# How many tiles of the gated pairs' experts go out with each state of the first two half-sequence scans

## The chip, the cores and the metric

The kernel runs on one core of a Trainium2 chip. The metric is device time in microseconds, the median of several runs. Engine names are those of the profile: PE (TensorE matmuls) and PEld (its weight loads), DVE (VectorE), ACT (ScalarE), POOL (GpSimd), and SP, the engine whose queue issues most of the transfers. Everything is in float32.

## What is computed

The reference is a network of four layers on an input of 4 sequences x 1024 positions x 128 features. Each layer is a mixer and a feed-forward, each followed by a residual sum and a layer norm. The change concerns the last three of these eight steps.

The feed-forward of the third layer ("gated pairs": each token goes to two of eight gated experts):

```python
logits = x @ router_w.T;  probs = softmax(logits)
weights, indices = top_k(probs, 2);  weights /= weights.sum() + 1e-6
gate, up = split(x @ w13[e]);  y_e = (silu(gate) * up) @ w2[e]
out = sum over the two chosen e of weight_e * y_e
```

The mixer of the fourth layer, a selective state recurrence ("Recurrence") with 256 channels and 16 states per channel:

```python
h = exp(d_l[:, :, None] * A) * h + (d_l * x_l)[:, :, None] * b_l[:, None, :]
y_l = einsum('ben,bn->be', h, c_l)      # for every position l
```

Its input is the rms-normed stream, put through a projection, a causal convolution of width 4 and a silu; `d_l` is a softplus. Its output is gated with the silu of a skip projection and projected back to 128 features.

The feed-forward of the fourth layer has eight experts of width 512, and every token's sum is over all eight with a gate that is zero for those outside its top-p set. The kernel computes all eight for every token.

## The kernel before

**The program.** A Python program writes out every instruction. A planner then makes, from that stream, one fixed order for each engine: an instruction's place in the stream is its priority, buffers are taken from pools with a fixed number of slots, and the planner's own timing decides which of the ready instructions comes next. On the chip each engine runs its list in that order. So the place at which a piece of work stands in the stream decides where it stands on PE, ACT, DVE, POOL and SP. Work that overlaps is written as Python generators, and the loop that calls `next` on them sets how they are mixed.

**The gated pairs' experts: `l2_ffn`, lines 1402 to 1437.** A router sorts each sequence's 2 x 1024 token copies by expert into at most 23 tiles of 128 rows (`NT2`), so the four sequences have 92 tiles. The scatter of rows is an indirect transfer issued by POOL (line 1383), 16 of them a sequence. `l2_ffn` is a generator that works as a pipeline over a step number t: at step t it loads rows for tile t+8 (once in four tiles, `xg`, line 1442), the expert's weights for tile t+4 (`wx`, 384 KB, line 1458, four buffers), transposes rows for tile t+2 (once in four), computes the hidden layer of tile t (`ph`, `sg`, `mh`, lines 1474 to 1494) and the output of tile t-2 (`py`, `ys`, line 1498), which SP stores once in four tiles. It then yields. A step whose rows belong to a sequence that isn't scattered yet does nothing but yield:

```python
while t + 8 < n and "put" not in units[max(t + 8, 0)]["st"]:
    ...
    yield
```

When the last tile of a sequence is out, `l2_combine` (line 1519) runs as a side generator, two of its steps to a step of tiles (one, once the tiles are all out or while they wait for rows): 8 indirect gathers on POOL (`yg`, line 1529), weighted sums on ACT and DVE, a norm, and the same again for the sequence's second half. `yg` has one buffer.

**The recurrence: `l3`, from line 1595.** Each sequence is cut into two halves of 512 positions, which makes 8 half sequences. For each, `l3_prepare` (line 1714) computes the channels, `dl` and `ud`, and two sets of 16 rows, b and c, which go to DRAM. Then `l3_scan` (line 1815) goes over the 16 states. For one state SP loads `bn` and `cn` (a row spread over 128 partitions, 256 KB each, line 1840, four buffers each); POOL multiplies `db` = `ud` x `bn` (line 1845); ACT makes the decay `da` (line 1849); DVE runs the scan over time in two pieces (line 1850); POOL multiplies `hc` = `db` x `cn` (line 1861); PE sums `hc` over the states into `pys` through an identity matmul. From the second sequence on, two states' `hc` are first added by a transfer that POOL issues (line 1865). `l3_sum` and `l3_finish` (lines 1874 and 1886) gate, project, norm and route a half sequence; `l3_finish` puts it on the list `todo`.

**The last layer's experts: `l3_experts`, `l3_ffn` (lines 1638 and 1955).** A half sequence on `todo` is taken up when it has been there for more than three states. Each of its eight experts takes six steps of the generator `work`: four for the hidden pieces (`ph`, `hh`), two for the output (`py`) and its gated sum into `h_acc`. The weights `wh` are 512 KB an expert.

**What mixes them.** With every state of a scan, the loop in `l3` calls one step of the finish of the half before (`end`), one step of the preparation of the next half (`nxt`), one step of the last sequence's scatter (`self.m2["rest"]`), the steps of tiles (`moe`), and three steps of `work`, or four once the tiles are through. The tiles, `l3_prepare`, `l3_finish` and the last layer's experts all take their PSUM banks from one pool of four (`ff`). Before a scan whose next half begins a new sequence, the loop drains `moe` until that sequence is combined.

Most of the loop's tiles are of the third and fourth sequences. By the trace's tile names the first 45 hidden layers run before the recurrence's pools are made, and 47 after.

Of the kernel before, what the change touches and what calls it, by code (L numbers as in the profile page):

```python
# [58 lines left out]
class Net:  # L59
# [1535 lines left out]
    def l3(self, moe, fp):  # L1595

        c3 = self.c3  # L1600
        halves = [dict(b=b, h=h) for b in range(B) for h in range(2)]
        for i, u in enumerate(halves):
            u["prev"] = halves[i - 1] if u["h"] else None
        halves[0] = dict(self.c3["first"], **{k: halves[0][k] for k in ("prev",)})
        for i, u in enumerate(halves[1:], 1):
            u["prev"] = halves[i - 1] if u["h"] else None
        work = self.l3_experts(fp)
        end = iter(())
        for i, u in enumerate(halves):
            nxt = iter(())  # L1610
            if i + 1 < len(halves):
                if halves[i + 1]["h"] == 0:
                    while "done" not in self.m2["st"][halves[i + 1]["b"]]:
                        next(moe)
                nxt = self.l3_prepare(halves[i + 1])
            for f in self.l3_scan(u):
                next(end, None)
                next(nxt, None)
                for k in range(1):
                    next(self.m2["rest"], None)  # L1620
                busy = next(moe, moe) is not moe
                if i == 0:
                    for k in range(1):
                        next(moe, None)
                for k in range(3 if busy else 4):
                    next(work)
                for v in c3["todo"]:
                    v["age"] += 1
            for f in chain(end, nxt):
                pass  # L1630
            end = chain(self.l3_sum(u), self.l3_finish(u))
        for f in end:
            next(work)
        c3["all"] = True
        for f in work:
            pass
# [566 lines left out]
```

## Time and profile before

| | us |
|---|---|
| time before, median of 3 runs | 2328.13 (2327.18 to 2331.37) |
| profiled execution, its own time | 2329.42 |
| span of that execution | 2327.6 |
| PE busy, share of the span | 1994.8 (86%) |
| DVE busy | 1348.4 (58%) |
| ACT busy | 1205.4 (52%) |
| POOL busy | 1024.8 (44%) |
| first `db` multiply of the first scan | 1386.6 |
| last `hc` multiply of the eighth scan ends | 2176.6 |

"Busy" is the time in which an engine has an instruction in flight; on PE this includes the pipeline, so a PE that is called busy need not be at its peak. Shares over the whole span mix the layers; what counts for this change is the stretch from 1340 on. A stretch's own table (busy time of each engine between two times) shows which engine sets the pace there, and a wait is read as: this instruction stood still so long, and that is what ended it. "SPq" and "POOLq" are the queues on which SP and POOL issue transfers: what waits at the head of such a queue holds all that stands behind it.

The first multiplies of the eight scans start at 1386.6, 1471.8, 1562.1, 1661.6, 1777.8, 1879.7, 1989.5 and 2089.5. The hidden layers of the last 47 tiles run from 1352 to 1696.

### The profile page before, as it was taken

The numbers are of one execution on the slowest core, as the hardware profiler recorded it, in microseconds if no ns is written. First come the engines' busy times: TensorE is split into PE (matmuls) and PEld (weight loads), VectorE is DVE, ScalarE is ACT, GpSimd is POOL, SyncE is SP. The second block draws the span as 40 slices with busy tenths as digits, with TensorE's granted clock in tenths as the row PEclk, the third lists the DMA queues.
The fourth block names the chain that finished last, engine by engine and source line by source line (L and its number), as shares of the span: only waits on it lengthen the run. The fifth ranks groups of instructions, "written<-read, shape, count | busy, mean of one in ns | idle before, by whom it ended". The sixth has DMA issues, their size and how long they took to land. (4 is left out here: it accounts for less than half of the span.)

```text
span 2327.6 us, 46367 instructions
## 1 busy us (share of the span) xinstructions
PE 1994.8 (86%) x17802; PEld 1395.0 (60%) x17802; DVE 1348.4 (58%) x3693; ACT 1205.4 (52%) x2617; POOL 1024.8 (44%) x813
## 2 busy tenths in 40 slices
PE   6667979979999999999979857678898989889888
PEld 3455655544477777787767654355655556546556
DVE  7458743433445554654655557767776767776421
ACT  6543433332244444454565556566668766666343
POOL 5000230000123244234143259989887887769300
PEclk9757979979999999999999978889999989899899
DMA  3000110014000010031222176457765666666421
GB/s 105 0 19 18 31 38 6 14 40 140 1 3 2 3 37 22 25 88 42 84 77 72 49 221 182 146 165 204 219 175 162 180 173 163 180 164 177 100 59 50
DMA packets 138701, 211.62 MB, mean 91 GB/s; under 512 B 18613, under 2 KB 75952, under 8 KB 138096
## 3 DMA queue, kind: packets, MB, share of 16 engines
q1 hardware_dynamic: 126192, 173.87, 24.7%
q0 software_dynamic: 12288, 34.79, 7.2%
q8 instruction: 140, 2.29, 0.4%
q14 instruction: 81, 0.66, 0.1%
HBM read 160.29 MB, written 23.16 MB: 79 GB/s over the span
## 5 line engine op out<-in xcount | busy, mean ns | idle before, releaser
L1059 POOL TENSOR_TENSOR qt<-r_q,sb_c_turn 128x256 f32<-128x256 f32 (+1 forms) x256 | 164.4, 663 | 446.7 <-ACT r_q L1051 441.0
L1861 POOL TENSOR_TENSOR hc<-db,cn 128x1024 f32<-128x1024 f32 x128 | 311.3, 2453 | 64.4 <-PE pys L127 20.4
L1845 POOL TENSOR_TENSOR db<-ud,bn 128x1024 f32<-128x1024 f32 x112 | 283.7, 2597 | 30.6 <-DVE pmv L159 19.1
L127 PEld LDWEIGHTS py<-wh,hh 128*128 128x128 f32 x2048 | 251.8, 196 | 67.8 <-issue 38.7
L127 PE MATMUL ph<-xT,wh 128*128 128x512 f32 x512 | 262.5, 634 | 21.7 <-ACT hh L1973 8.0
L127 PE MATMUL py<-wh,hh 128*128 128x128 f32 x2048 | 257.2, 280 | 13.0 <-ACT hh L1973 10.1
L1973 ACT ACTIVATE hh<-ph,sb_cols 128x512 f32<-128x512 f32 x256 | 170.6, 682 | 146.2 <-PE ph L127 119.9
L1117 DVE TENSOR_TENSOR a<-pa_m,sb_c_near 128x256 f32<-128x256 f32 x256 | 96.6, 419 | 204.2 <-PE pa_m L127 204.2
L1074 ACT ACTIVATE kN<-kp_mo,sb_c_trig 128x128 f32<-128x128 f32 x448 | 130.2, 372 | 131.9 <-PE kp_mo L131 122.1
L1849 ACT ACTIVATE da<-dl,aneg 128x512 f32<-128x512 f32 x224 | 153.2, 689 | 84.1 <-DVE db L1850 83.3
L127 PE MATMUL pys<-hc,sb_c_ident 128*128 128x512 f32 x320 | 162.0, 636 | 24.6 <-POOL hc L1861 15.0
L1850 DVE TENSOR_TENSOR_SCAN db<-da,carry,db 128x512 f32<-128x512 f32 x128 | 156.8, 1266 | 25.9 <-ACT da L1849 12.5
L127 PEld LDWEIGHTS ph<-xT,wh 128*128 128x128 f32 x512 | 93.5, 202 | 115.0 <-issue 65.7
L1850 DVE TENSOR_TENSOR_SCAN db<-da,db 128x512 f32<-128x512 f32 x128 | 149.1, 1205 | 14.3 <-ACT da L1849 8.2
L1989 DVE SCALAR_TENSOR_TENSOR h_acc<-py,gt,h_acc 128x128 f32<-128x128 f32 x256 | 71.9, 342 | 140.4 <-PE py L127 140.4
L127 PE MATMUL pqk<-xT,wE 128*128 128x256 f32 x512 | 137.7, 393 | 8.2 <-ACT coT L1193 4.2
L127 PEld LDWEIGHTS pys<-hc,sb_c_ident 128*128 128x128 f32 x320 | 61.7, 206 | 90.0 <-issue 59.1
L127 PEld LDWEIGHTS pqk<-xT,wE 128*128 128x128 f32 x512 | 89.4, 195 | 22.1 <-DVE cv L1036 8.1
L729 POOL DMA_INDIRECT orows<-o,ix x20 | 18.9, 946 | 185.3 <-DVE o L727 158.8
L131 PE MATMUL pt<-sb_c_ident,xN 128*128 128x128 f32 x224 | 54.5, 345 | 52.1 <-ACT xN L174 33.9
L1193 ACT COPY coT<-pt 128x512 f32<-128x512 f32 x64 | 37.6, 587 | 114.7 <-PE pt L131 114.7
L127 PE MATMUL po<-ht,wD 128*128 128x512 f32 x192 | 93.7, 595 | 0.0
(457 smaller groups left out, 4342.4 us busy)
## 6 DMA issues: line engine op xcount, KB each, us to landing
wx<-in_wF SPq DMA_DIRECT2D x92, 384.0 KB, 3.4
bn<-rows SPq DMA_DIRECT2D x128, 256.0 KB, 4.9
cn<-rows SPq DMA_DIRECT2D x128, 256.0 KB, 4.5
wh<-in_wH SPq DMA_DIRECT2D x64, 512.0 KB, 3.9
hc<-hc POOLq DMA_DIRECT2D x48, 512.0 KB, 7.1
xrows<-zero SPq DMA_DIRECT2D x4, 1472.0 KB, 12.4
xg<-xrows SPq DMA_DIRECT2D x20, 256.0 KB, 3.1
yrows<-ys SPq DMA_DIRECT2D x20, 256.0 KB, 3.3
```

The costliest lines, as they stand in the source:

```text
L127: return self.nc.tensor.matmul(out=out, lhsT=lhsT, rhs=rhs, start=start, stop=stop)
L131: self.nc.tensor.transpose(out, in_, self.ident[0:n, 0:n])
L1059: nc.gpsimd.tensor_mul(u["qt"][:, m, a:], u["q"][:, a:], c2["turn"][:, m, o + a : o + 2 * P])
L1074: self.nc.scalar.activation(u["kN"][:, c, m, :], pk[:, c, :], AF.Copy, scale=trig[:, k, m : m + 1])
L1117: nc.vector.tensor_mul(u["a"][:, i, :, :], pa[i], self.c2["near"][:, None, :].to_broadcast([P, 2, P]),)
L1193: nc.scalar.copy(oT, pt)
L1845: nc.gpsimd.tensor_mul(db, ud, bc[0])
L1849: nc.scalar.activation(da, dl[:, ec, :], AF.Exp, scale=aneg[:, j : j + 1])
L1850: nc.vector.tensor_tensor_scan(db[:, ec, :], da, db[:, ec, :], carry[:, ec, n : n + 1] if h else 0.0, ALU.mult, ALU.add,)
L1861: nc.gpsimd.tensor_mul(hc, db, bc[1])
L1973: nc.scalar.activation(ht, ph, AF.Relu, bias=self.col("h_b1", i=e * NK + k))
L1989: nc.vector.scalar_tensor_tensor(acc[:, c, :], py[:, c, :], gt[:, c, e : e + 1], acc[:, c, :], ALU.mult, ALU.add,)
```

## The change

In the loop of `l3`, i is the number of the half sequence, 0 to 7. Before, one step of tiles goes out with each state, and one more in half sequence 0. After, three more go out in half sequence 0 and one more in half sequence 1: four and two steps a state, and one in the others, as before.

```diff
                 for k in range(1):
                     next(self.m2["rest"], None)
                 busy = next(moe, moe) is not moe
-                if i == 0:
-                    for k in range(1):
-                        next(moe, None)
+                for k in range((3, 1)[i] if i < 2 else 0):
+                    next(moe, None)
                 for k in range(3 if busy else 4):
                     next(work)
```

## Prediction

> **What bounds the kernel now.** I read first the page's busy shares, then a table of busy time by stretch, then waits and queues inside the stretches that the change reaches. A "scan" below is the sixteen states of one half sequence; I cut the trace where each scan's first POOL multiply `db` starts. The columns are time, then busy PE, PEld, DVE, ACT, POOL, then the granted clock, the DMA share and GB/s.
>
> ```profile
> 1386.60:1471.80 85.20, 59.90 (x212) 35.12 (x212) 58.46 (x85) 51.59 (x116) 82.70 (x41) 0.81 0.56 171
> 1471.80:1562.10 90.30, 64.33 (x278) 40.29 (x276) 67.77 (x123) 53.69 (x107) 77.20 (x39) 0.91 0.56 167
> 1562.10:1661.60 99.50, 83.55 (x440) 59.11 (x441) 74.61 (x139) 72.40 (x152) 87.42 (x48) 0.95 0.70 196
> 1661.60:1777.80 116.20, 102.44 (x504) 66.80 (x503) 84.32 (x171) 80.97 (x149) 96.95 (x58) 0.96 0.63 170
> 1777.80:1879.70 101.90, 92.61 (x426) 57.84 (x425) 76.30 (x147) 75.11 (x142) 86.99 (x45) 0.95 0.70 187
> 1879.70:1989.50 109.80, 99.76 (x489) 65.08 (x487) 77.42 (x153) 71.96 (x118) 82.60 (x43) 0.95 0.66 178
> ```
>
> These are scans one to six. In scan one POOL is busy 82.70 of 85.20 us: it sets the pace. In scan two it is busy 77.20 of 90.30, and PE stands idle 26 us. From scan three PE has the last layer's experts too (seven in ten or more of the stretch is PE), and scans three and four are the long ones, with the gated pairs' tiles still in them. Scan four alone is 14.3 us longer than scan five, which has no such tile.
>
> Next the tile stream, in the second scan, by its lines, and two dense pieces of PE's order of time in the third:
>
> ```profile
> L127 PE MATMUL ph<-xgT,wx 128*128 128x128 f32 x96 | 13.9, 291 | 4.4 <-DVE db L1850 2.9 <-ACT ys L1510 1.5
> L127 PE MATMUL py<-wx,mh 128*128 128x128 f32 x48 | 8.0, 292 | 9.8 <-ACT dl L1810 6.5 <-DVE mh L1494 3.2
> L1529 POOL DMA_INDIRECT yg<-yrows,di x8 | 7.6, 950 | 2.3 <-issue 1.5 <-DMA cn<-rows 0.3 <-DVE mh L1494 0.3
> ...
> 1577.35 1.05 PE L127 MATMUL ph<-xgT,wx 128*128 128x128 f32 x8
> 1578.24 0.61 PE L127 MATMUL py<-wx,mh 128*128 128x128 f32 x4
> ```
>
> Twelve tiles cost PE 13.9 + 8.0 us in the second scan, 1.8 us each; in the dense pieces a tile takes about 1.5 us (0.9 to the next group's start, and 0.6). Then what the SP queue waits for in that scan, and POOL's stall in the fourth:
>
> ```profile
> SPq L1458 <- PE py L127: 36.5, 12, 10.0
> SPq L1840 <- POOL db L1845: 8.4, 5, 1.9
> ...
> 1755.64 1.08 POOL L1529 DMA_INDIRECT yg<-yrows,di  x1 [7.65 <-ACT xN L174]
> ```
>
> The first says that SP, which also loads `bn` and `cn` for the scan, stood 36.5 us in front of loads of `wx` until PE had finished with an older buffer. The last is the fourth sequence's second group of gathers, for which POOL stood still for 7.65 us in scan four.
>
> **The change part by part.** It adds and removes no instruction: every tile, scan, gather and load stays. What moves is counted from the loops. By the trace 47 tiles' hidden layers read the banks of the last layer's pools, so the generator enters the loop at its step 45 of 92. In scan one it gets to step 60 and then returns empty, because step 61 asks for rows of the fourth sequence, whose writes are marked done only in the first state of scan two.
>
> *Scan one.* The 16 steps are given out in 4 states where it was 8; the other 48 calls do nothing (16 before). About 10 tiles (84 matmuls of `ph<-xgT`, 8 a tile) ran after the scan's first multiply, until 1445. They can come forward, but POOL, at 97%, hides it: a gain of at most the 2.5 us that POOL is idle. Behind them stand `l3_prepare` of half two, whose `ud` was ready at 1438.8 and not used before 1471.8: 33 us of cover. Tiles in a burst follow each other by 2.85 us (activations `sg` at 1387.4, 1390.9, 1393.5, 1396.2, 1398.8), so sixteen last some 46 us, and cover remains. The loads of `wx` come sooner too, in front of `bn` and `cn` on SP; four buffers of each lie ahead. I take 0; bounds -2.5 and +5 (one late `bn`, the size of the 4.9 us that POOL once waited for one).
>
> *Scan two.* Steps 61 to 92 are given out here, where it was 61 to 76: 16 tiles more. PE: 16 x 1.8 = 29 us on 64.33, 93 in all at the scan's clock, and with dense pieces 16 x 1.5 = 24, or 88. DVE: 16 x (0.42 + 0.41), 13 us on 67.77, so 81. ACT: 16 x (0.36 + 0.25 + 0.12), 12 us on 53.69. DMA: 16 x (384 KB of weights, 64 of rows in, 64 out) = 8 MB on the 15 MB that 167 GB/s give in 90.3 us; in 98 us that is 237 GB/s, a little over the 221 of the fullest slice on the page. POOL: the third sequence's second eight gathers (1564.7 to 1574.4, 9.7 us) now belong here, on 77.20: 87. None of them alone exceeds 98 us, but POOL's 13 us of idle remains for the same reasons (scans and `wx`). I take 98, +8 us. Bounds: 0, if all goes into PE's idle time and the gathers into POOL's; and +22, worked out under the first rival. Behind the extra tiles stands `l3_prepare` of half three: `ud` at 1530.6, used at 1562.1, 31 us of cover; nine more tiles ahead of its last step at 2.85 are 26 us, so it just holds.
>
> *Scan three.* Out go 13 of its 16 tile steps and eight gathers; in come the fourth sequence's sixteen (given out in scan four before). PE loses 13 x 1.5 = 20 us of 83.55, but the experts that lag behind (5 of the 8 given out had run by 1661.6) move up. POOL has 87.42 - 7.6 + 15.6 = 95.4 of 99.5 and takes PE's place. I take -2; bounds -4 (POOL without a gap, 95.4) and +8 (the 7.65 us stall comes here with the gathers).
>
> *Scan four.* Out go the last tiles, sixteen gathers (15.6 us of POOL) and the 7.65 us stall. What is late next is PE with eight experts, as in scan five: 101.9. So -14; bounds -20 (POOL's 97.0 - 15.6, and the 15 us that scan five's POOL is idle) and -4 (experts given out at four a state from state 5 on, 11 more calls, about 2 experts, 14 us of PE if they are there to run; what limits them is that half k is routed only near state 9 of scan k+1).
>
> *Later.* Scan six had 1.25 halves of experts in it (from the counts of `h_acc`) because of the lag; with the lag smaller I take -4 for scans five and six, bounds -10 and +6 (a static order that falls otherwise: 20.8 us lie between the sixth scan's last multiply and the seventh's first). The end after the eighth scan, 151 us with two halves of experts, is as before.
>
> Sum: 0 + 8 - 2 - 14 - 4 = -12 us. The profiled execution took 2329.4 us (2327.6 of span and 1.8 around it), 1.3 over the median, so the forecast goes 12 under the median: 2316.
>
> A rule that weighs against this: the Trainium skill, "Perfetto Trace Analysis", section "Identifying the Most-Contended Engine", says that busy matmul time is no measure of how near PE is to its limit, and that the share of weight loads is. In scan four that share is 66.80 of 116.20, 57%, and POOL at 83% would be the engine to relieve. By that rule only POOL's moves count: about +8 in scan two, +8 in scan three, -16 in scan four, and the sum is 0, 2328. I hold to the rows, since in scan four ACT waits on PE.
>
> **The rivals.**
> 1. *SP couples the scan to the tiles, slower.* Two tiles a state at 2.85 us each are 5.7 us; a state of scan two takes 90.3/16 = 5.6. If a tile needs more than about 3.1 us (98/32), SP stands before `wx` longer than four `bn` last, and the scan runs at the tiles' pace. For: the 36.5 us row. Against: in that scan POOL's own waits name a load for 2.3 us only. The twelve `sg` of scan two lie from 1486.4 to 1553.1; seven of their eleven gaps are under 8 us and make 24.3 us together, 3.5 each. At that, 32 tiles take 112 us: +22 there. With +8 in scan three, -14 in four and nothing later, +16: 2344.
> 2. *It washes out.* Experts are given out only when a half has been routed, and scans five to eight and the end keep their order; what scans three and four win, scan two and the later gaps give back: +8, -2, -8, +2 is 0, 2328, between 2323 and 2333.
> 3. *All of it is hidden.* Scan two stays at 90 to 92 since PE and POOL had 26 and 13 us idle, scan three goes to 95, scan four to 100, scan six to 100: -27, 2301.
>
> **How the numbers follow.** Forecast 0.45 (own range 2308 to 2323), rival one 0.30, rival two 0.13, rival three 0.12. The likeliest is the forecast, 2316. The range has to reach into rival three and over most of rival one, whose bounds run from 2336 to some 2355: 2296 to 2348. No change means within 0.2%, 4.7 us, about what this kernel's times can tell apart: 2323.5 to 2332.8. Faster: nearly all of the forecast (0.42), rival three, a little of rival two (0.02): 0.56. Same: 0.03 + 0.09 + 0.01 = 0.13, the rest of it 0.31 slower.
>
> **What would show it.** Last `sg` of the tiles near 1580, not 1695.5. Scan two's stretch between 94 and 102 us with POOL idle no more than 15; above 110, with SP's wait on `PE py` grown, is rival one. Scan four within 5 us of scan five, with no gathers in it. If scans two to four together are no shorter than 306 us, the forecast's middle is wrong; if they are shorter and the end is not, the gaps before the later scans took it back. The prediction would be wrong altogether if the static order, which is made anew from the changed stream, puts `l3_prepare` behind the tiles: then a gap on POOL stands before scan two or three.

## The result, and the profile after

| | before | after |
|---|---|---|
| median of 14 runs each, side by side | 2331.62 us | 2339.56 us |
| ratio, with its 95% interval | | 1.0033 [1.0016, 1.0049] |
| profiled execution, its own time | 2329.42 us | 2347.61 us |
| its span | 2327.6 us | 2345.8 us |

The change makes the kernel slower by a third of a per cent, 7.9 us. I had forecast 12 us the other way.

The profiled execution of after is the longest of its 14 runs, 8 us above their median, so not all of the 18.2 us between the two spans is the change's. The lists that the five engines work through are the same in both kernels up to the loop of the recurrence. Counted in the two programs, with semaphore waits left out, these are the first 7480 of PE's 9501 rows, 2416 of DVE's 3645, 1467 of ACT's some 2540, 472 of POOL's 818 and 377 of SP's 922. Yet the 39th tile's output copy `ys`, which is still in that common part, comes at 1333.8 us before and at 1341.0 after. One kernel that was profiled twice, on two chips (`four_one` below), had it at 1336.9 and at 1341.9. Those 7.2 us are not counted here: below, times in the loop are taken from this `ys`, and called "in" (us since it). From it to the end the loop took 993.9 us before and 1004.9 after, +11.0. Two more profiles with the same lists as these two (the kernels `before_three` and `after_three` below) took 997.4 and 1002.3, +4.9. So the loss inside the loop has one sign in both pairs and no sharp size, and a split of one profile is good to some 3 us.

First the table by stretch of after, the six lines that answer to the ones shown for before. A stretch runs from one scan's first `db` to the next scan's. The columns are time, busy PE, PEld, DVE, ACT, POOL, clock, DMA share, GB/s.

```profile
1394.70:1480.50 85.80, 59.55 (x228) 36.77 (x229) 61.16 (x92) 54.08 (x119) 80.70 (x40) 0.81 0.56 165
1480.50:1583.50 103.00, 76.06 (x324) 48.95 (x323) 79.41 (x149) 67.00 (x136) 89.52 (x50) 0.85 0.60 177
1583.50:1693.30 109.80, 94.05 (x471) 62.64 (x470) 74.80 (x143) 76.64 (x158) 95.19 (x55) 0.95 0.64 179
1693.30:1795.50 102.20, 91.09 (x424) 56.27 (x422) 77.09 (x150) 73.84 (x128) 85.08 (x44) 0.95 0.69 181
1795.50:1906.50 111.00, 96.96 (x471) 63.94 (x469) 75.73 (x149) 70.48 (x130) 82.12 (x43) 0.95 0.64 171
1906.50:2009.40 102.90, 88.66 (x416) 56.16 (x416) 74.06 (x139) 68.63 (x114) 81.30 (x41) 0.91 0.61 167
```

Against before the scans are +0.6, +12.7, +10.3, -14.0, +9.1 and -6.9; the seventh and eighth -1.1 and -0.9; the end after the last multiply +0.2. POOL is about as busy in scans two and three as I had worked out (89.5 and 95.2; I had 87 and 95.4), but it still stands idle 13.5 and 14.6 us in them, as it did before (13.1 and 12.1). The gain of scan four is as large as forecast.

Next, what SP waits for in scan two, and POOL's gap before scan six (the start and length of POOL's instructions, and in brackets the idle time before with what ended it):

```profile
SPq L1458 <- PE py L127: 29.0, 12, 6.1
SPq L1839 <- POOL hc L1860: 13.5, 8, 2.8
```

```profile
1883.38 0.88 POOL L1864 DMA_DIRECT2D hc<-hc  x1 [0.30 <-POOL hc L1860]
1906.49 6.94 POOL L1844 TENSOR_TENSOR db<-ud,bn 128x1024 f32<-128x1024 f32 x3 [22.23 <-DVE pmv L159]
```

SP's wait before `wx` went down, from 36.5 to 29.0 us. The second fence is a gap that before did not have at this place: POOL stands 22.2 us in front of scan six because that half's `ud` is not there (DVE starts to write its last part 564.7 in, the scan starts 565.5 in). Before, that scan followed with no gap, and the long one, 19.1 us, stood before scan seven.

Last, PE's order of time at the border of scans one and two, where a first delay lies:

```profile
1477.78 0.61 PE L127 MATMUL ph<-xgT,wx 128*128 128x128 f32 x4
1478.22 0.61 PE L127 MATMUL py<-wx,mh 128*128 128x128 f32 x4
1478.67 5.32 PE L127 MATMUL pys<-hc,sb_c_ident 128*128 128x512 f32 x12
1487.56 2.93 PE L127 MATMUL pys<-hc,sb_c_ident 128*128 128x512 f32 x4 [3.58 <-POOL hc L1860]
1492.17 2.08 PE L127 MATMUL pys<-hc,sb_c_ident 128*128 128x512 f32 x2 [1.68 <-POOL hc L1860]
1494.04 0.64 PE L127 MATMUL po<-sb_s_e,xs 128*128 128x128 f32 x2
...
1498.59 0.39 PE L127 MATMUL ph<-xgT,wx 128*128 128x128 f32 x2
```

`ph<-xgT` is a tile. Between the tile at 1477.8 and the next one at 1498.6 PE adds up the last states of scan one (`pys`, to the group at 1487.56) and stands still 3.58 us for POOL's last `hc` of that scan. The `pys` from 1492.17 on, with the second wait, are already scan two's. The next fence, POOL at the same border, shows why the last `hc` is late:

```profile
1475.88 2.42 POOL L1844 TENSOR_TENSOR db<-xT,bn 128x1024 f32<-128x1024 f32 x1
1478.22 2.38 POOL L1860 TENSOR_TENSOR hc<-db,cn 128x1024 f32<-128x1024 f32 x1
1480.53 4.68 POOL L1844 TENSOR_TENSOR db<-ud,bn 128x1024 f32<-128x1024 f32 x2
1485.14 2.37 POOL L1860 TENSOR_TENSOR hc<-db,cn 128x1024 f32<-128x1024 f32 x1
```

The two `db<-ud` at 1480.5 belong to scan two (scan one's read `xT`). They stand in POOL's list ahead of the last `hc` of scan one, at 1485.1. In before the list has all of scan one's `hc` first:

```profile
1469.54 2.33 POOL L1861 TENSOR_TENSOR hc<-db,cn 128x1024 f32<-128x1024 f32 x1
1471.84 9.25 POOL L1845 TENSOR_TENSOR db<-ud,bn 128x1024 f32<-128x1024 f32 x4
```

The program did not ask for this: the planner makes the lists anew from the changed stream, and from the start of the loop to nearly the end those of after and before differ.

### The profile page after: what moved, and what is told of

Same layout as the page of the kernel before. It is cut to its first block, busy times and chain, and to the rows that moved or that the text cites. A ratio compares the mean times of both kernels' runs of the same rounds, so it can differ in the third digit from the quotient of the medians.

```text
span 2345.8 us, 46395 instructions
## 1 busy us (share of the span) xinstructions
PE 2000.6 (85%) x17802; PEld 1397.9 (60%) x17802; DVE 1349.2 (58%) x3693; ACT 1210.3 (52%) x2621; POOL 1024.2 (44%) x813
## 5 line engine op out<-in xcount | busy, mean ns | idle before, releaser
L127 PE MATMUL py<-wh,hh 128*128 128x128 f32 x2048 | 254.8, 277 | 10.5 <-ACT hh L1972 10.3
L1972 ACT ACTIVATE hh<-ph,sb_cols 128x512 f32<-128x512 f32 x256 | 170.3, 681 | 138.1 <-PE ph L127 111.6
L127 PE MATMUL pqk<-xT,wE 128*128 128x256 f32 x512 | 138.1, 393 | 8.3 <-ACT coT L1193 4.3
```

The lines of the kernel that those rows point to most:

```text
L127: return self.nc.tensor.matmul(out=out, lhsT=lhsT, rhs=rhs, start=start, stop=stop)
L1972: nc.scalar.activation(ht, ph, AF.Relu, bias=self.col("h_b1", i=e * NK + k))
```

## The experiments

Each ratio below is to the kernel before on the same chip, with its 95% interval. The first four kernels and the last four ran on chips where before takes 2328.7 and 2327.4 us, the middle four on one where it takes 2368.8.

**One part of the change at a time.** My first two theories were named "backlog" (the tiles handed out early stand in front of the preparations and the finish of the halves in the common bank pool) and "gathers" (two sequences' gathers on POOL in scans two and three lengthen them). A third, "any new order", said that the planner's new lists decide, whatever is moved. The first kernel has only the four steps a state in half 0 (its diff is to before), the second only the two in half 1 (its diff is to after).

```diff
-                if i == 0:
-                    for k in range(1):
-                        next(moe, None)
+                for k in range((3, 0)[i] if i < 2 else 0):
+                    next(moe, None)
```

> The first half of the change alone: four tile steps a state in scan one, one in scan two. Theory 'backlog' (the loss comes from scan two's sixteen further steps, behind whose tiles the finish of the second half sequence and the preparation of the fourth have to wait): ratio to before 0.999 to 1.001, the second half sequence's skip projection psk within 10 us of the last sum of its scan as before. Theory 'gathers' (the loss comes from the combine's gathers lying in scans two and three): the same, since no gather moves. Theory 'any new order' (each new static order moves the end by several us, whatever is changed): off by 0.2% or more, either way.

Measured: 2315.39 us, ratio 0.9937 [0.9924, 0.9951].

```diff
-                for k in range((3, 1)[i] if i < 2 else 0):
+                for k in range((1, 1)[i] if i < 2 else 0):
                     next(moe, None)
```

> The second half alone: two steps a state in scan one as before, and two in scan two. Theories 'backlog' and 'gathers': 1.002 to 1.005, the whole loss; psk of the second half sequence comes only after the last tile, near 1615 on the clock of before, where it was 1576. Theory 'any new order': no relation to the changed kernel's 1.0033.

Measured: 2323.12 us, ratio 0.9979 [0.9969, 0.9989].

Each part alone makes the kernel faster, and together they make it slower. `four_one` should not have moved by "backlog" or "gathers", and it is the fastest kernel of all. `two_two` has the last tile out 266.4 in and all sixteen gathers in scans two and three, as in after, and should have been slower; it is faster. Both theories fall. What is left has to be something that only the two parts together bring about, or the lists themselves.

**The buffers of the preparation.** Another cause could be that a preparation cannot start until the half before it has let go of the two buffers of `xnT` and `xs3`. These kernels give halves 3 and 6 a third pair (that of the first half, which is free by then).

```diff
-        xnT = at("xnT", [P, 512])
+        third = (2 * b + h) in (3, 6)
+        xnT = c3["first"]["xnT"] if third else at("xnT", [P, 512])
 ...
-        xs = at("xs3", [P, 2, 512])
+        xs = c3["first"]["xs"] if third else at("xs3", [P, 2, 512])
```

> The kernel before, where the third and the sixth half sequence after the first take the first one's xs3 and xnT, which lie unused, so that three buffers of each go round instead of two and a preparation no longer waits for the finish two half sequences back. Theory 'backlog': the gap of 19 us on POOL before the seventh scan and that of 11 before the eighth shrink; 0.990 to 0.998. If these waits only take turns with PE's experts: 0.998 to 1.002.

Measured: 2330.68 us, ratio 0.9997 [0.9984, 1.0011].

> The changed kernel with the same three buffers. Theory 'backlog' (the late finish holds the buffers, and so the sixth scan's start): the 22 us gap of POOL before the sixth scan goes, and the ratio to before comes within 0.2% of that of before with three buffers. Theory 'gathers': the changed kernel stays 0.3% above before with three buffers, since scans two and three still hold the gathers.

Measured: 2339.01 us, ratio 1.0040 [1.0028, 1.0052].

The lists of all five engines come out the same as without the third pair, the times too, and POOL's gap before scan six is again 22.2 us. It does not come from these buffers. The two kernels also serve as a second measurement of before and after, with the same verdict.

**Moving something else in the stream.** If only the lists decide, small moves elsewhere should change the time too. Two theories are set against each other in what follows: "collide" (each part gains, and the two get in each other's way at the border of scans one and two) and "later order" (the lists from scan three on set the time, whatever leads to them). `after_prep2` and `before_prep2` give two steps of the next half's preparation out with each state of the first scan; `three_two` hands out three and two steps of tiles; `before_swap` calls the preparation ahead of the finish.

```diff
                 next(nxt, None)
+                if i == 0:
+                    next(nxt, None)
```

> The changed kernel, four and two steps, but in scan one the preparation of the second half sequence also gets two of its steps a state, so that its first projections stand after 4 and 8 tiles of PE's list, not after 12 and 16. Theory 'two parts collide' (each part alone uses up cover that the other needs: four a state pushes the preparation of half two back by some 20 us, and the two-a-state tiles then meet it in scan two): the ratio falls to that of the second part alone, 0.996 to 1.000. Theory 'any new order': no relation, anywhere from 0.993 to 1.005; theory 'backlog of tiles in scan two alone': stays at 1.003.

Measured: 2365.37 us, ratio 0.9979 [0.9965, 0.9992].

> Control: the kernel before with the same two preparation steps a state in scan one. There the preparation was ready 33 us ahead of its use. Theory 'two parts collide': 0.998 to 1.002. Theory 'any new order': off by more than 0.2% either way.

Measured: 2360.96 us, ratio 0.9973 [0.9958, 0.9987].

```diff
-                for k in range((3, 1)[i] if i < 2 else 0):
+                for k in range((2, 1)[i] if i < 2 else 0):
```

> Three steps a state in scan one, two in scan two: the dose between the second part alone (0.998) and the changed kernel (1.003). The preparation's projections stand after 9 and 15 tiles of PE's list (6 and 10 in the second part alone, 12 and 16 in the changed kernel). Theory 'two parts collide': between them, 0.999 to 1.003. Theory 'any new order': need not lie between.

Measured: 2363.93 us, ratio 0.9979 [0.9961, 0.9997].

```diff
-                next(end, None)
                 next(nxt, None)
+                next(end, None)
```

> A change that moves no work: the kernel before with the step of preparation called ahead of the step of finish in each state, not behind it. It measures what a mere new order is worth. Theory 'two parts collide': 0.999 to 1.001. Theory 'any new order': off by 0.2 to 0.6% either way, as large as all the other differences here.

Measured: 2367.03 us, ratio 0.9995 [0.9981, 1.0009].

`after_prep2` is the change itself with one preparation step more, and its loss is gone. Its lists, those of `three_two` and those of `two_two` are the same from before the first multiply of scan two to the end (PE's last 1862 rows, DVE's 1096, ACT's 947, at least 331 of POOL's, 423 of SP's), and the three have one ratio, 0.9979. The changed kernel shares only PE's last 586 rows with them. So three different ways of handing out tiles that lead to one late list have one ratio, though the last kernel but one below shows that a common late list is not enough. `before_prep2` speaks against "collide" as the only cause: the step helps before too, which has neither part of the change. `before_swap` shows that not every new order moves the time.

**The border on POOL.** The next kernel is the changed one with one rule for the planner: the first `db` of scan two stands behind the last `hc` of scan one. `four_one_pool` puts the same rule into the fastest kernel, whose POOL list also has two `db` ahead of that `hc`.

```diff
-            nc.gpsimd.tensor_mul(db, ud, bc[0])
+            with self.tc.issue_after(c3["lasthc"]) if (b, h, n) == (0, 1, 0) else nullcontext():
+                nc.gpsimd.tensor_mul(db, ud, bc[0])
 ...
-            nc.gpsimd.tensor_mul(hc, db, bc[1])
+            c3["lasthc"] = nc.gpsimd.tensor_mul(hc, db, bc[1]).ins
```

> The changed kernel, where POOL's list must hold all sixteen hc multiplies of scan one before the first db of scan two. In the changed kernel two db stand in front of the last hc, the last sum of scan one is 6.6 us later than in the second part alone (counted from the last tile before the loop), the next tiles as well, and the first expert 13 us. Theory 'two parts collide' (the loss is made by scan two): the last sum comes 5 to 7 us earlier, the first expert by 8 or more, and the ratio falls from 1.003 to 0.997 to 1.001. Theory 'later order' (the time is set by which static order the planner makes for scans three to eight): since that order is again another one, anywhere from 0.993 to 1.005.

Measured: 2320.31 us, ratio 0.9969 [0.9955, 0.9984].

> The first part alone (four and one steps; 0.9937) with the same rule for POOL's list. With it all five engines have, from the third scan on, exactly the list of the kernel before. Theory 'later order': the gain goes, 0.998 to 1.002. Theory 'two parts collide' (what counts is scans one and two, and they lose a delay here): 0.990 to 0.995.

Measured: 2330.39 us, ratio 1.0007 [0.9990, 1.0023].

"Later order" is right about `four_one_pool`. "Collide" is near for `after_pool` (the last sum 4.3 us earlier, the first expert 9.5, and a ratio of 0.9969 where 0.997 to 1.001 was expected) and wrong for `four_one_pool`. In `after_pool` POOL's list is that of after for 511 rows, up to this border. POOL's order of time there, to be held against the fence of after:

```profile
1473.41 2.43 POOL L1861 TENSOR_TENSOR hc<-db,cn 128x1024 f32<-128x1024 f32 x1
1477.51 2.35 POOL L1861 TENSOR_TENSOR hc<-db,cn 128x1024 f32<-128x1024 f32 x1 [1.67 <-DVE db L1850]
1479.81 9.27 POOL L1845 TENSOR_TENSOR db<-ud,bn 128x1024 f32<-128x1024 f32 x4
```

The last `hc` of scan one is now ahead of scan two's `db`, though POOL stands idle 1.7 us for it. Its scans two to five, in the table by stretch:

```profile
1479.80:1581.50 101.70, 78.14 (x358) 54.54 (x359) 76.94 (x152) 67.36 (x142) 84.84 (x48) 0.85 0.59 180
1581.50:1692.90 111.40, 101.80 (x504) 67.44 (x504) 82.35 (x157) 78.72 (x159) 97.84 (x56) 0.97 0.63 179
1692.90:1784.30 91.40, 79.99 (x360) 49.21 (x359) 71.91 (x135) 67.79 (x116) 81.23 (x41) 0.96 0.67 179
1784.30:1882.80 98.50, 91.23 (x452) 59.33 (x450) 73.80 (x144) 69.71 (x130) 85.42 (x44) 0.99 0.72 198
```

Scans two and three are as long as in after, but more is done in them: PE is busy 179.9 us in the two, against 170.1. Eight experts are through when scan four starts, against six, and scan four takes 91.4 us instead of 102.2, scan five 98.5 instead of 111.0. The delay, point by point (us in; each row up to the fourth is the start of the last instruction of what it names, and an expert is four sums into `h_acc`):

| | before | after | after_pool | two_two | four_one | four_one_pool |
|---|---|---|---|---|---|---|
| last sum of scan one | 143.4 | 151.8 | 147.5 | 145.2 | 151.3 | 144.0 |
| last tile's output | 375.0 | 279.0 | 269.6 | 266.4 | 374.5 | 374.9 |
| first expert done | 237.5 | 278.4 | 268.9 | 265.7 | 240.6 | 237.5 |
| first half's eight experts done | 354.6 | 363.4 | 349.0 | 348.7 | 357.2 | 354.2 |
| from the row above to the end | 639.3 | 641.4 | 631.5 | 634.5 | 623.9 | 640.5 |

After loses 8.8 us up to the eighth expert and 2.1 behind it. (The second pair of profiles has 356.7 and 363.1, then 640.7 and 639.2: again the early part carries the loss.) With the one rule, the early part is 14.4 us shorter and ends below before's. That the rule takes the loss away is shown; that all 14.4 us come from the two `db` is not, since the lists behind the border are planned anew as well.

The same rule in `four_one` costs that kernel its whole gain. It wins 3.0 us early, as it should, and then loses 16.6, because the lists behind it change: from scan three on they are before's (PE's last 1806 rows, DVE's 990, ACT's 854, POOL's 296, SP's 387). So the tiles of half 0 do not by themselves make the gain of `four_one`: they are still given out at four a state, and the time is that of before. The scans that differ most are the fourth and the fifth. First those two of `four_one`, then of `four_one_pool`:

```profile
1670.70:1779.70 109.00, 100.47 (x497) 65.14 (x495) 82.91 (x168) 81.76 (x149) 94.28 (x55) 0.95 0.66 187
1779.70:1875.50 95.80, 85.61 (x406) 53.92 (x407) 75.50 (x146) 72.21 (x137) 84.86 (x43) 0.97 0.73 191
```

```profile
1667.20:1783.30 116.10, 102.37 (x491) 66.03 (x490) 82.97 (x170) 79.48 (x147) 97.02 (x58) 0.94 0.63 170
1783.30:1887.40 104.10, 94.37 (x426) 58.20 (x425) 77.70 (x148) 75.57 (x144) 87.06 (x45) 0.93 0.68 182
```

Another 8.4 us lie at the end after the eighth scan: 142.4 us in `four_one`, 150.8 in `four_one_pool`. In return `four_one_pool` has scans two and three of 87.1 and 99.4 us, where `four_one` has 90.5 and 104.8.

**The last two.** One combines `four_one` with the extra preparation step, the other is `four_one` again.

> The first part alone with two preparation steps a state in scan one: a second way to the same later lists as before, by another early part. Theory 'later order': 0.998 to 1.002. Theory 'two parts collide': 0.990 to 0.995.

Measured: 2336.47 us, ratio 1.0035 [1.0024, 1.0047].

> The first part alone once more, beside the two runs above on one chip: 0.992 to 0.996 under either theory, if what was measured on the other chip holds here.

Measured: 2315.64 us, ratio 0.9946 [0.9926, 0.9967].

`four_one` repeats on another chip, and its loop took 981.2 us where it took 981.1 the first time. `four_one_prep2` is a miss for both theories. Its lists are before's from within scan one on (PE's last 1902 rows), so I had expected before's time. Its profile shows 365.9 us up to the eighth expert, 11 more than before, with a scan one that lasts to 148.0 in (138.1 before); behind that it is 629.5, which is 10 us less than before with the same late lists, and its profiled execution took 5.6 us less than its median. What the extra step costs in the first scan, and why the same late list took less time there, stays open.

**The granted clock.** The kernels also differ a little in the mean granted clock of their runs. On the chip of the first four it is 0.923 in `four_one` and `two_two`, 0.921 in before and 0.918 in `after_three`; on that of the last four it is 0.923 in `four_one_again`, 0.921 in before and `after_pool`, 0.920 in `four_one_pool` and 0.917 in `four_one_prep2`. Within one kernel on one chip, a run whose clock is 0.001 lower took 1.1 us longer on average (230 runs on record with their clock). By an estimate from that slope, the clock goes with about 3 of the 10 us by which `after_three` is longer than before and with 5 of the 9 us of `four_one_prep2`, and with nothing of the gain of `after_pool`; no result whose interval excludes 1 would change its sign. Whether the lists bring the lower clock about or it comes by itself, no run here tells.

## Why the prediction was wrong

*What bounds the kernel.* Reading the stretches one by one was right for scan one (0 forecast, +0.6) and for scan four (-14 forecast, -14.0 measured, 102.2 us against the 101.9 of before's scan five that I had named as its limit; eight experts ran in each of the two).

*Scan two, +8 forecast, +12.7 measured.* POOL's and DVE's busy times came near what I had worked out (89.5 for 87, 79.4 for 81), PE's did not: 76.1 us where I had 88 to 93. The term priced 28 tiles in this scan by their busy time. Between its start and end the count of tiles goes from 67 to 83: sixteen, where before had twelve. So DVE's agreement is luck: four tiles are 3.3 us of its 11.6 more, and 5.7 are six more pieces of the scans over time that fell inside this stretch. The scan grew by 12.7 us for four tiles more and eight gathers, at a granted clock of 0.85 where before had 0.91. Handing a step out is not running it: PE idled 26.9 us here, as it did before (26.0), above all in front of POOL's `hc` and ACT's `ys`. Busy time gave a lower bound of this scan, and the idle time in it did not take up the further work.

*Scan three, -2 forecast, +10.3 measured: this is the step that failed.* "Out go 13 of its 16 tile steps" was true of the stream and not of the chip: nine tiles were still in the scan, and their last `sg` came 273.1 in and not near 246 (1580 on before's time axis). The experts that were to move up hardly did: six were through when scan four began, where before had five. POOL had the 95.2 us of work that I had counted, but did not close its gaps; 14.6 us of idle remain, and the scan takes 109.8, not 97.5. All the kernels that move the gathers here have such a scan three (111.4 in `after_pool`, 110.3 in `two_two`). Those two are faster than before all the same, so it is not the loss by itself. What sets after apart from them is what is through when scan four begins: six experts, not eight (`after_pool`) or seven and a half (`two_two`). All fourteen profiles have 32 experts through when scan seven begins, and scans four to six together took 11.7 to 12.2 us for each expert left to them: 316.0 us for 26 in after, 327.9 for 27 in before, 288.1 for 24 in `after_pool`, 294.4 for 24.5 in `two_two`. So the tiles taken out of scans three and four pay only as far as experts come earlier for it, and in after only one did.

*Later, -4 forecast, +2.2 measured for scans five and six.* The scan with ten experts only moved: before, it was scan six (109.8 us), in after it is scan five (111.0 us), which is 9.1 us longer, with the 22.2 us that POOL stands before scan six; scan six has eight and is 6.9 us shorter. By the start of scan seven the lag is the same, 32 experts through in both. The bound of +6 that I gave for "a static order that falls otherwise" was of the right kind.

The sum by these steps is +0.9 (start of scan one), +0.6, +12.7, +10.3, -14.0, +2.2, -2.0 (scans seven and eight) and +0.2: +10.9, the loop's 11.0 but for rounding.

*What would show it wrong.* Scans two to four together took 315.0 us, and I had named 306 as the limit from which the forecast's middle is wrong. The last clause, that the order made anew puts `l3_prepare` behind the tiles, did not come true as written: the preparation of half three was ready 21 us before scan three, where it had 31 before. What fell behind the tiles is the second half's finish (`l3_finish`). Its skip projection ran at 1576.5 before, among the tiles. In after it stands behind the last of them:

```profile
1619.22 0.61 PE L127 MATMUL py<-wx,mh 128*128 128x128 f32 x4
1619.67 2.74 PE L127 MATMUL ph<-xT,wh 128*128 128x512 f32 x6
1622.24 1.02 PE L127 MATMUL psk<-xnT,sb_s_in 128*128 128x512 f32 x2
```

This is not the loss by itself: `two_two` and `after_pool`, which are faster than before, have it behind their last tile too. And the gap on POOL that I said would follow before scan two or three came before scan six. I had put the new order as a closing condition with no price. By the experiments it was the main case: the changed kernel and the same with one preparation step more lie 0.5% apart (1.0033 and 0.9979), as much as the whole gain that I forecast, and I had no row that could tell which list the planner would make.

*The rivals.* Rival one had the sign, and the wrong mechanism: SP's wait went down to 29.0 us, and scan two did not reach 110. Rival two gave 2323 to 2333; the median is 2339.6, and the two measurements of the changed lists (1.0033, and 1.0040 [1.0028, 1.0052]) leave little room for that. Rival three is off in scans two, three and five. The rule that I weighed (the Trainium skill, "Perfetto Trace Analysis", section "Identifying the Most-Contended Engine") names two measures of PE's limit, its share of peak matmul work (MFU) and the busy share of its weight loads; I used the second alone. With it POOL was the engine to watch in scan four, and the sum was 0. That sum had +8 in scan three, where +10.3 was measured, and -16 in scan four, where -14.0 was measured. It is nearer than mine, but `four_one` and `four_one_pool`, with the same work on each engine and 0.6% apart, show a part of the time that no share of an engine tells.

## What to carry to other kernels

Where a planner lays out each engine's list from the order of the stream, a move in the stream is two changes: the one meant, and a new list. Compare the lists before explaining a time, and try the change in parts and with one harmless step added or moved; if the ratio jumps about as it did here (0.9937, 0.9979, 1.0033, and 1.0007 with one rule), the tuning lever is the list, and the parts do not add up. Of the kernels tried, `four_one` (four steps a state in half 0 and one in all others) is the one to keep, 0.9937 and 0.9946 in two measurements, though only as long as nothing else in the stream is moved.

## What the runs showed of the chip that was not expected

The same lists before the loop took between 1333.5 and 1342.4 us on chips where before has a median of 2328 us, with a mean granted clock of 0.922 (`before_three`) and 0.915 (`after_three`) in that stretch, so a single profile's span can hide or invent 9 us, as much as this whole change. On the chip of the middle four kernels, before took 2368.8 us, 1.7% more than on the others, at a mean granted clock of 0.912 where they had 0.921, and the 39th tile's output came at 1356.7 to 1364.0. The ratio of `four_one` held between the two other chips (0.9937 and 0.9946); on this one, of the kernels run elsewhere, only before was measured, so whether ratios hold there is not shown.
